# A float residual added by a transposing TensorE pass instead of an identity product

## The chip, the cores and the metric

The kernel runs on one core of a Trainium2 chip. The metric is the device time of one execution in microseconds (us). TensorE (PE, with its weight loads PEld) multiplies, VectorE (DVE) and ScalarE (ACT) work on elements, GpSimd (POOL) too, and SyncE (SP) mostly issues DMA transfers.

## The reference

Four layers follow each other on x of shape (4, 128, 128, 128), all in float32. Each is x = x + layer(groupnorm(x)).

```python
x = x + _L0_conv_ref(_gn(x), ...)   # deformable 3x3 convolution, ReLU
x = x + _L1_conv_ref(_gn(x), W)     # scan over rows: new = row + relu(conv1d(carry, W))
x = x + _L2_conv_ref(_gn(x), ...)   # three products: itself, sum over width, sum over height
x = x + _L3_conv_ref(_gn(x), ...)   # triangle product, below
```

The last layer is the one that matters here:

```python
xn = layer_norm(x, norm_g, norm_b)
left = (xn @ left_w + left_b) * sigmoid(xn @ lgate_w + lgate_b)
right = (xn @ right_w + right_b) * sigmoid(xn @ rgate_w + rgate_b)
out_gate = sigmoid(xn @ ogate_w + ogate_b)
out = einsum('bkjd,bkid->bijd', left, right)
out = layer_norm(out, onorm_g, onorm_b) * out_gate
return out @ to_out_w + to_out_b
```

## The kernel before, in words

The deformable layer runs to about 3050 us of the span, the scan over rows from there to 3931 us, and `message_and_triangle`, which holds layers 2 and 3, from there to the end. Only the last is touched.

In it one image is worked on after the other, in three parts.

- `taken_in(b)`, a generator, reads layer 1's output in strips of eight rows (`x2c`), forms layer 2 into `X` (L1276, L1282, L1285), writes `X` to memory as `x3T` in the layout [channel, row, column], and then normalises it in place: product with a centring matrix (L1316), squares, means (L1331), a round trip through memory for the row factors (`stdT`, `rstd`, `rwide`), and a multiplication on DVE (L1354).
- `multiplied(b)` makes left and right with their gates (L1369, L1374, L1375), the output gate, which goes to memory as `gateT` (L1382 to L1389), and the triangle product into `T` (L1393, L1397).
- `given_out(b, T)`, a generator, yields the output in 32 groups of four rows. DVE takes the statistics of `T` (L1409 to L1423); ACT and POOL normalise to `u` (L1438, L1434). Then, per group: a gate is loaded into `gate` (L1446) and a part of `x3T` into `x3` (L1448); TensorE transposes `u` (L1451); ACT scales it to `y` (L1453); POOL multiplies by the gate (L1454). The sum `po` is then made in PSUM, for each of four columns j: the residual `x3[:, j]` (L1457) opens the sum, the product of `y[:, j]` and `outw` (L1460) closes it. ACT copies `po` into the same `gate` buffer (L1461), and SP writes it out (L1462).

`x3` comes with channels on the partitions, and the output has rows there; so the residual has to be turned on its way into the sum. The kernel before does this with a plain product: `x3[:, j]` as stationary operand and the identity as moving one.

`gate`, `x3`, `y` and `u` have two buffers each; `po` and the transposes share four PSUM banks (`one_ps`); `T` and `X` have one buffer each.

The loop at the end of `message_and_triangle` takes in image 0, and then for each image calls `multiplied(b)` and steps through `given_out(b)` with two steps of `taken_in(b + 1)` after each group. The last image's output thus has nothing beside it. On each engine the instructions are laid in an order that a planner works out from the program; in the trace, the first L1457 of a group stands before the transposes (L1451) of the following one. SP issues the DMAs of all three parts in one queue, in order.

Of the kernel before, what the change touches and what calls it, by code (L numbers as in the profile page):

```python
# [1154 lines left out]
def message_and_triangle(tc, c, x2T, counted, w2, w3, out, x3T, gateT, stdT):  # L1155
# [10 lines left out]
    with ExitStack() as ctx:  # L1166
# [76 lines left out]
        def single(shape=(P, 512)):  # L1243
            return ps_s.tile(list(shape), F32, name="one_ps", tag="one_ps")
# [155 lines left out]
        def given_out(b, T):  # L1400

            prod = T[:, 0:NQ].rearrange("p q d j -> p (q d) j")
            JS = 2 * JB

            def factors(j0):

                st = two.tile([P, JS, 6], F32, name="st")
                for j in range(JS):
                    nc.vector.bn_stats(st[:, j, :], prod[:, :, j0 + j])  # L1409

                both = two.tile([P, JS, 2], F32, name="both")
                nc.vector.tensor_tensor(both, st[:, :, 1:3], st[:, :, 4:6], ALU.add)
                apart = two.tile([P, JS], F32, name="apart")
                nc.vector.tensor_tensor(apart, st[:, :, 1], st[:, :, 4], ALU.subtract)
                nc.vector.tensor_tensor(apart, apart, apart, ALU.mult)
                rs = two.tile([P, JS], F32, name="rs")
                nc.vector.scalar_tensor_tensor(
                    rs, apart, P / 4.0, both[:, :, 1], ALU.mult, ALU.add
                )
                nc.scalar.activation(rs, rs, AF.Sqrt, bias=c.eps, scale=1.0 / P)  # L1420
                nc.vector.reciprocal(rs, rs)
                nm = two.tile([P, JS], F32, name="nm")
                nc.vector.scalar_tensor_tensor(nm, both[:, :, 0], -0.5, rs, ALU.mult, ALU.mult)  # L1423
                return rs, nm

            ready = factors(0)
            for j0 in range(0, S, JB):
                if j0 % JS == 0:
                    rs, nm = ready
                u = two.tile([P, JB, P], F32, name="u")  # L1430
                for j in range(JB):
                    of, k = prod[:, :, j0 + j], j0 % JS + j
                    if j % 4 == 3:
                        nc.gpsimd.tensor_scalar(  # L1434
                            u[:, j], of, rs[:, k : k + 1], nm[:, k : k + 1], ALU.mult, ALU.add
                        )
                    else:
                        nc.scalar.activation(  # L1438
                            u[:, j], of, AF.Identity, bias=nm[:, k : k + 1], scale=rs[:, k : k + 1]
                        )  # L1440
                if j0 % JS == 0 and j0 + JS < S:
                    ready = factors(j0 + JS)
                for h in range(0, JB, 4):
                    j1 = j0 + h
                    gate = two.tile([P, 4, S], F32, name="gate")
                    nc.sync.dma_start(gate, gateT[b, :, j1 : j1 + 4, :])  # L1446
                    x3 = two.tile([P, 4, S], F32, name="x3")
                    nc.sync.dma_start(x3, x3T[b, :, j1 : j1 + 4, :])  # L1448
                    pt = single((P, 4, P))
                    for j in range(4):  # L1450
                        nc.tensor.transpose(pt[:, j], u[:, h + j], c.ident)  # L1451
                    y = two.tile([P, 4, P], F32, name="y")
                    nc.scalar.activation(y, pt, AF.Identity, bias=obcol, scale=ogcol)  # L1453
                    nc.gpsimd.tensor_tensor(y, y, gate, ALU.mult)  # L1454
                    po = single((P, 4, P))
                    for j in range(4):
                        nc.tensor.matmul(  # L1457
                            po[:, j], lhsT=x3[:, j, :], rhs=c.ident, start=True, stop=False
                        )
                        nc.tensor.matmul(po[:, j], lhsT=y[:, j], rhs=outw, start=False, stop=True)  # L1460
                    nc.scalar.copy(gate, po)  # L1461
                    nc.sync.dma_start(out[b, :, j1 : j1 + 4, :], gate)  # L1462
                    yield
# [3 lines left out]
        for b in range(B):  # L1467
            T = multiplied(b)
            after = taken_in(b + 1) if b + 1 < B else iter(())
            for _ in given_out(b, T):  # L1470
                next(after, None)
                next(after, None)
            for _ in after:
                pass
# [75 lines left out]
```

## Time and profile before

| | |
|---|---|
| median of three runs | 5704.68 us (5692.88 to 5705.37) |
| profiled execution, its own time | 5716.77 us |
| its span, first to last instruction | 5715.0 us |
| mean granted TensorE clock | 0.952 |
| PE, PEld busy | 5055.9 us, 4359.9 us |
| DVE, ACT, POOL busy | 3207.3, 2556.8, 1162.6 us |
| L1457 records, weight loads as well | 1024 each, from 4279 to 5711 us |
| L1451 records | 512, from 4279 to 5700 us |

The layer-3 part by stretches, with TensorE's busy time and the mean granted clock:

| stretch, us | what runs | PE busy, us | clock |
|---|---|---|---|
| 4279 to 4463 | output of image 0, intake of image 1 | 143.6 | 0.93 |
| 4463 to 4530 | last groups of image 0, products of image 1 | 51.8 | 0.87 |
| 4530 to 4695 | products of image 1 | 153.5 | 0.98 |
| 5112 to 5296 | output of image 2, intake of image 3 | 145.0 | 0.92 |
| 5365 to 5517 | products of image 3 | 151.5 | 1.00 |
| 5517 to 5715 | output of image 3 alone | 119.6 | 0.72 |

A row of the groups names the line, engine and operation, the tiles written and read, the shapes and the count; then busy time and mean duration of one; then the engine's idle time ahead of them and what ended it. Records of TensorE overlap: a matmul's duration is longer than the step to the next one. The chain of work that ended last is followed back from the last instruction to what released each step. A row of the timeline has start, length, engine, line, operation, and, in brackets, idle time before it.

### The profile page before, as it was taken

The page shows a single profiled execution, that of the slowest core. Times are in us where ns is not written, and L with a number is a line of the kernel's source. Part 1 is how long each engine was busy: PE and PEld are TensorE (multiplying, and loading weights), DVE is VectorE, ACT ScalarE, POOL GpSimd, SP SyncE. Part 2 cuts the span into 40 slices and gives each one's busy share as a digit, 9 for nine tenths or more (in the row PEclk, how much of TensorE's full clock was granted, in tenths as well). Part 3 has the DMA queues.
Part 4 walks back from the last instruction along what each step waited for, and adds up shares of the span by engine and source line. Part 5 has one row for each costly group of instructions (what it writes and reads, how often), then busy time and mean ns, then how long its engine had stood idle before and what let it go on. Part 6 is the DMA issues. An engine that isn't in the chain of part 4 may idle for free. (4 is left out here: it accounts for less than half of the span.)

```text
span 5715.0 us, 163429 instructions
## 1 busy us (share of the span) xinstructions
PE 5055.9 (88%) x69432; PEld 4359.9 (76%) x69432; DVE 3207.3 (56%) x8190; ACT 2556.8 (45%) x5243; POOL 1162.6 (20%) x1013
## 2 busy tenths in 40 slices
PE   2898999999999999899998999997797887887886
PEld 1787788787887888788997999996474774774775
DVE  4666666666666666655555666666446245345350
ACT  1554454544545445445442333331445445446444
POOL 4222222201212012221000111112104204214112
PEclk9999999999999999999998999999999999999987
DMA  4776566665666756556442222222417317327324
GB/s 150 155 166 148 128 148 133 154 132 114 148 135 144 142 103 146 130 125 130 87 92 79 78 87 77 77 87 75 149 49 238 129 66 235 118 79 230 111 70 134
DMA packets 1273820, 710.73 MB, mean 124 GB/s; under 512 B 845645, under 2 KB 1112174, under 8 KB 1263862
## 3 DMA queue, kind: packets, MB, share of 16 engines
q1 hardware_dynamic: 1243538, 658.56, 46.1%
q10 hardware_dynamic: 29540, 41.60, 2.1%
q8 instruction: 549, 8.99, 0.7%
q14 instruction: 193, 1.58, 0.1%
HBM read 417.28 MB, written 282.55 MB: 122 GB/s over the span
## 5 line engine op out<-in xcount | busy, mean ns | idle before, releaser
L606 PE MATMUL conv_ps<-ring,wdef 128*128 128x192 f32 (+2 forms) x7632 | 1295.4, 319 | 5.8 <-DVE x1c L576 4.8
L514 DVE TENSOR_TENSOR m<-t_ps,tent 128x390 f32<-128x390 f32 x1548 | 806.9, 557 | 785.1 <-ACT tent L512 769.2
L606 PEld LDWEIGHTS conv_ps<-ring,wdef 128*128 128x128 f32 x7632 | 1141.5, 194 | 125.3 <-issue 64.0
L512 ACT COPY tent<-t_ps 128x390 f32<-128x390 f32 x1560 | 691.4, 487 | 652.6 <-PE t_ps L498 642.4
L498 PE MATMUL t_ps<-parts_of,spread 57*64 57x99 bf16 (+1 forms) x12384 | 741.7, 275 | 167.2 <-DVE m L514 145.0
L523 PE MATMUL v_ps<-m,pixels 60*64 60x108 f32 (+1 forms) x22704 | 813.7, 265 | 18.4 <-DVE m L514 8.8
L498 PEld LDWEIGHTS <-spread 57*64 57x64 bf16 x12480 | 577.5, 125 | 311.8 <-issue 264.5
L523 PEld LDWEIGHTS v_ps<-m,pixels 60*64 60x64 f32 x22704 | 674.0, 137 | 68.7 <-DVE m L514 23.1
L549 ACT COPY ring<-v_ps 128x432 f32<-128x432 f32 x1032 | 505.7, 525 | 445.1 <-PE v_ps L523 444.4
L420 POOL TENSOR_TENSOR off<-off,koff 72x512 f32<-72x512 f32 x128 | 162.7, 1271 | 1761.8 <-DVE off L417 1761.8
L1369 PEld LDWEIGHTS pair_ps<-wcat,X 128*128 128x128 f32 x4096 | 474.3, 192 | 52.3 <-POOL X L1356 23.2
L1369 PE MATMUL pair_ps<-wcat,X 128*128 128x128 f32 x4096 | 495.9, 279 | 19.8 <-POOL X L1356 18.2
L1375 DVE TENSOR_TENSOR T<-pair_ps,sig 128x512 f32<-128x512 f32 x256 | 266.8, 1043 | 424.1 <-ACT sig L1374 415.5
L1110 PEld LDWEIGHTS own_ps<-diff,wconv 128*128 128x128 f32 x4064 | 494.4, 191 | 13.2
L1110 PE MATMUL own_ps<-diff,wconv 128*128 128x128 f32 x4064 | 495.2, 273 | 0.0
L506 PE MATMUL t_ps<-parts_of,spread 57*64 57x130 bf16 x9288 | 454.2, 225 | 0.0
L1150 POOL TENSOR_TENSOR sum_h<-sum_h,x2c 128x512 f32<-128x512 f32 x128 | 162.5, 1269 | 1137.9 <-DVE x2c L1136 680.4
L438 DVE SCALAR_TENSOR_TENSOR parts<-off,parts 72x512 bf16<-72x512 f32 x384 | 296.1, 772 | 150.7 <-ACT parts L430 145.0
L1460 PE MATMUL one_ps<-outw,y 128*128 128x128 f32 x1024 | 247.6, 334 | 122.5 <-POOL y L1454 122.4
L1068 ACT ACTIVATE rowT<-x1T_ps,t_x,s_x 128x128 f32<-128x128 f32 x512 | 207.7, 568 | 313.2 <-PE x1T_ps L1064 313.2
L1460 PEld LDWEIGHTS one_ps<-outw,y 128*128 128x128 f32 x1024 | 195.2, 239 | 174.5 <-POOL y L1454 172.7
L506 PEld LDWEIGHTS <-spread 57*64 57x64 bf16 x9312 | 318.8, 108 | 0.1
(183 smaller groups left out, 6930.0 us busy)
## 6 DMA issues: line engine op xcount, KB each, us to landing
pixels<-tab SPq DMA_DIRECT2D x688, 123.8 KB
parts_of<-off SPq DMA_DIRECT2D x1032, 55.7 KB
off<-parts SPq DMA_DIRECT2D x64, 891.0 KB
tab<-rows SPq DMA_DIRECT2D x384, 128.0 KB
xin<-in_x_dram SPq DMA_DIRECT2D x128, 256.0 KB
x<-x1c SPq DMA_DIRECT2D x32, 1024.0 KB
x1rows<-x SPq DMA_DIRECT2D x128, 256.0 KB
x2T<-x2c ACTq DMA_DIRECT2D x128, 256.0 KB
```

The source lines that it names most:

```text
L438: nc.vector.scalar_tensor_tensor(parts[:, NSPLIT + i, h : h + RO, 2 : S + 2], off, 0.0, part, ALU.is_gt, ALU.mult,)
L498: nc.tensor.matmul(tp[h : h + HALF, 0, 0:n].rearrange("p (r c) -> p r c", c=PADW)[:, :, i:PADW:RX], lhsT=spread[0:k, kx // 2, i, h : h + H ...
L506: nc.tensor.matmul(tp[h : h + HALF, 1, i * PADW : (i + 1) * PADW], lhsT=spread[HALF : HALF + k, kx // 2, first + i, h : h + HALF], rhs=src ...
L512: nc.scalar.copy(tent[:, 0:n], tp[:, 0, 0:n])
L514: nc.vector.tensor_tensor(m, *pair, ALU.mult)
L523: nc.tensor.matmul(to[p1 : p1 + HALF], lhsT=pix[p0 : p0 + LANES, xb, :], rhs=m[p0 : p0 + LANES, :, RX * xb : RX * xb + w], start=True, sto ...
L549: nc.scalar.copy(to, bodies[side])
L606: nc.tensor.matmul(pc[:, at : at + rows, x0:x1], lhsT=wdef[:, side, k, :], rhs=v[:, :, k if v.shape[2] == NK else kx, x0 + kx : x1 + kx], ...
L1110: nc.tensor.matmul(own[:, n], lhsT=wt[:, 2 * j + n, :], rhs=diffs[h][:, n, :, j : j + V], start=False, stop=(n == 1 and j == NJ - 1),)
L1369: nc.tensor.matmul(pj[:, j], lhsT=X[:, j0 + j, :], rhs=wcat[:, q * 4 * DQ : (q + 1) * 4 * DQ], start=True, stop=True,)
L1375: nc.vector.tensor_tensor(T[:, q : NQ + 1 : NQ - q, :, j0 : j0 + JB], pj[:, :, 0 : 2 * DQ].rearrange("p j (n d) -> p n d j", n=2), sig.rea ...
L1460: nc.tensor.matmul(po[:, j], lhsT=y[:, j], rhs=outw, start=False, stop=True)
```

## The change

One argument is added to the first of the two matmuls that make `po`. The operands, the order, the buffers and everything else stay.

```diff
                     po = single((P, 4, P))
                     for j in range(4):
                         nc.tensor.matmul(
-                            po[:, j], lhsT=x3[:, j, :], rhs=c.ident, start=True, stop=False
+                            po[:, j], lhsT=x3[:, j, :], rhs=c.ident, start=True, stop=False,
+                            is_transpose=True,
                         )
                         nc.tensor.matmul(po[:, j], lhsT=y[:, j], rhs=outw, start=False, stop=True)
```

With it the pass is a transpose of `x3[:, j]` with the identity as the other operand, the form of L1451, and its result is still what the following product adds to.

## The prediction

> **What bounds the kernel now.** I read the page for the whole, then the groups of instructions by line and shape for the prices, the timeline for the true spacing of TensorE's passes, the chain of work that ended last for what lies on the path, and the waits of SP's queue for what is late next.
>
> ```profile
> span 5715.0 us, 163429 instructions
> ...
> PEclk9999999999999999999998999999999999999987
> ```
>
> Each digit is a fortieth of the span, 143 us. The edited line runs from 4279 us on, so only the last eleven or so slices matter: 1436 us after the scan. In the last one and a half the granted clock falls: the windows query gives 0.72 for 5517 to 5715 us, where it gives 0.92 for the earlier output stages and 0.98 for the products between them. A mean of 0.72 between full and half speed means about 55% of that stretch at half speed.
>
> ```profile
> L1460 PE MATMUL one_ps<-outw,y 128*128 128x128 f32 x1024 | 247.6, 334 | 122.5 <-POOL y L1454 122.4
> L1457 PE MATMUL one_ps<-ident,x 128*128 128x128 f32 x1024 | 238.3, 321 | 53.1 <-DMA x<-x3T 51.5 <-ACT gate L1461 1.4
> ...
> L1451 PE MATMUL one_ps<-ident,u 128*128 128x128 f32 x512 | 89.6, 299 | 41.1 <-ACT u L1438 41.0
> ```
>
> The counts are what to see. The source calls each of the three lines 512 times (4 images, 32 groups, 4 columns). L1451, which already transposes, has 512 records; L1457 and L1460, plain float products of the same size, have 1024: two passes each, with two weight loads. The mean of 321 ns is the latency of one pass; passes overlap, so it is not the price. The price is the step from one weight load to the next:
>
> ```profile
> 4482.27 0.55 PEld L1460 LDWEIGHTS one_ps<-outw,y 128*128 128x128 f32 x2
> ...
> 4482.69 0.87 PEld L1451 LDWEIGHTS one_ps<-ident,u 128*128 128x128 f32 x4
> ...
> 4483.54 0.55 PEld L1457 LDWEIGHTS one_ps<-ident,x 128*128 128x128 f32 x2
> ...
> 4483.97 0.87 PEld L1451 LDWEIGHTS one_ps<-ident,u 128*128 128x128 f32 x4
> ```
> ```profile
> 4430.22 0.30 PEld L1460 LDWEIGHTS one_ps<-outw,y 128*128 128x128 f32 x2
> ...
> 4430.44 0.47 PEld L1451 LDWEIGHTS one_ps<-ident,u 128*128 128x128 f32 x4
> ...
> 4430.88 0.30 PEld L1316 LDWEIGHTS pair_ps<-X,cs 128*128 128x128 f32 x2
> ```
>
> The first block is at half clock: two product passes take 4482.69 - 4482.27 = 0.42 us, four transposes 0.85 us, two identity passes 0.43 us: 0.21 us a pass, whatever its kind. The second is at full clock: 0.22 us for two, 0.44 us for four: 0.11 us a pass. Going from products to transposes and back adds nothing in either block.
>
> ```profile
> by line: issue 11.6%; POOL zc L1276 9.7%; DMA rwide<-stdT 9.4%; DVE X L1285 9.3%; DMA gate<-gateT 8.7%; POOL y L1454 6.4%; PE one_ps L1460 4.6%; DVE st L1409 3.8%; ACT u L1438 3.8%; PE one_ps L1457 3.4%; DMA stdT<-rstd 3.2%; DMA out_dram<-g
> ```
> ```profile
> by line: DMA gate<-gateT 21.3%; PE one_ps L1460 20.3%; PE one_ps L1457 13.1%; POOL y L1454 10.3%; DMA out_dram<-gate 9.0%; issue 8.9%; ACT u L1438 4.3%; ACT gate L1461 4.2%; DVE st L1409 4.2%; SPq L1462 1.0%; POOL u L1434 0.5%; PE one_ps L1
> ```
>
> The first is the chain from 4279 to 4463 us, where the output of image 0 runs beside the intake of image 1; it is spread over POOL, DVE and DMA. The second is the last image alone, 5517 to 5715 us: no engine is full, and the path is a ring. One turn of it:
>
> ```profile
> 5599.57 1.27 POOL y L1454
> 5600.89 0.80 PE one_ps L1460 x2
> 5601.68 0.43 PE one_ps L1457 x2
> 5602.11 0.43 PE one_ps L1460 x2
> ...
> 5604.32 0.59 ACT gate L1461
> 5604.93 2.58 DMA out_dram<-gate
> 5607.53 3.15 DMA gate<-gateT
> 5610.84 1.27 POOL y L1454
> ```
>
> There are two gate buffers. A gate is loaded, multiplied on POOL, gone through on TensorE, evicted into the same buffer, written out, and only then is the next gate loaded. TensorE's passes of a group stand in full on this ring, 11.3 us a turn, at half clock. SP's queue, in the stretch from 5510 us, shows the second tie:
>
> ```profile
> SPq L1448 <- PE one_ps L1457: 92.5, 18, 17.1
> SPq L1446 <- DMA out_dram<-gate: 29.6, 21, 2.4
> ```
>
> SP waits with a load of x3 until the last identity product of an earlier group lets the buffer go; the write of the output and the next gate loads are queued behind it.
>
> **What the Trainium skill says.** "TensorE: Matmul & The Clock Gate", Terms, says that the weight load and matmul have a transpose mode, four times faster for FP32. The trace shows half of that: one pass in place of two, each at the same step. The same page, Part 4, puts a transpose in a kernel at about 275 ns and says that transposes do not count as TensorE activity for the full clock. L1451's median record of 273 ns agrees with the first; no run here shows the second, and I keep it as a risk. Its Part 1 gives some 3.4 us of busy time before the clock rises; at 5600.88 us passes start at 0.21 us and reach 0.11 us at about 5604, which agrees. "PSUM — Partial Sum Buffer" (rule 2 on accumulation) says that a float transpose sets the written bits as a product does, so the product can add onto it; the trace before has no such pair.
>
> **The change part by part.** It removes one pass and one weight load from each of 512 identity products. All L1457 weight loads, by the step to the following load, have medians of 112 ns (663 of them) and 213 ns (306), mean 143 ns: 512 x 0.143 = 73 us less TensorE work. That is the ceiling of the direct gain, not the gain. No DMA, buffer, engine or wait is added or moved in the source.
>
> Unshown: a transpose opening a sum that a product then closes. From below: no extra, as at every change between L1451 and products above; no reason speaks for a gain beyond the removed pass. From above: one lost pass per pair, which eats the saving entirely. I take no extra, and keep the upper end as a rival.
>
> What lies on the path: L1457's share of the chain by stretch, times its length. Last image: 13.1% x 198 = 25.9 us. Output beside intake: 3.4% x 184 = 6.3, 4.0% x 195 = 7.8 and 3.4% x 194 = 6.6 us. The remaining groups beside the next image's products (about 68 us each): 7.5%, 7.1% and 9.0%, so 5.0, 4.9 and 6.2 us. The mixed stretches sum to 36.8 us. Half goes: 13.0 us and 18.4 us.
>
> The last image, checked from the ring: after y is ready a group runs 8 product passes and 6 identity passes (the first identity product went ahead); 3 of 14 go, 0.64 us at 0.213. Turns that go through the second group as well lose 6 passes, 1.28 us at half clock, or 0.64 us where the clock had risen. Sixteen turns of 0.64 to 1.28 us are 10 to 20 us; as both buffers have to come round, I keep 13. What is late next there is the gate load itself (3.15 us) and y on POOL: in this turn the second y ends at 5602.87 us (1.27 us from 5601.60) and TensorE, which came to it at 5603.83, would come 0.64 us earlier, so POOL keeps some 0.3 us of slack; much more would not all count.
>
> In the mixed stretches I take 70% of 18.4, 13 us: POOL's zc, DVE's X and the round trips of the row factors stand there beside the ring, and take over some of what is freed. The 70% is a choice; 0% and 150% (x3 buffers free earlier, so SP's queue moves up) are its ends.
>
> Sum: 26 us. The profiled execution took 5716.8 us (1.8 us around the span), which gives 5690.8. It lies 12 us above the median of the runs shown; taken from that, 5704.7 - 26 = 5679 us.
>
> **Rivals.** (a) Hidden in the mixed stretches: only the last image gains, 6 to 13 us, about 5695. For it: no line holds over 12% of that chain; against it: SP waits for L1457 and L1460 there too. (b) Larger: with the queue of SP moving up, the mixed stretches give back more than the chain shows, 50 us in all, 5655. For it speaks that T can't be overwritten before the last group is out. (c) Slower: the order on TensorE is not that of the source (the first identity product of a group stands ahead of the transposes of the next), so a planner that weighs durations lays it, and shorter passes can make it lay SP's queue differently in the mixed stages. The price of one bad place is on the chain:
>
> ```profile
> 4367.01 11.00 DMA gate<-gateT
> ```
>
> A gate load of 11.0 us where others take about 3.2: 8 us. From four of these more (over 26 / 8 = 3.3) the gain is gone; two per mixed stage, six, give 48 - 26 = 22 us slower, 5727. Against it: no duration elsewhere changes. (d) The transpose opening a sum costs a pass more, or is still run as two: 0, 5705.
>
> A clock that sags because transposes do not count would cost part of the last image's 13 us and leaves the case in (a).
>
> **How the numbers follow.** Forecast (17 to 37 us less) 0.50; (a) 0.24; (b) 0.13; (c) 0.09; (d) 0.04. About 0.3%, 17 us, is what a measurement of this kernel can tell from no change. Faster is the forecast and (b), 0.63; same (a) and (d), 0.28; slower (c), 0.09. The range goes from 5648 (most of b) to 5702 (nearly all of a); outside are (c), (d) and the tail of (b), some 0.17.
>
> **What would show it.** L1457 with 512 records, steps of 0.11 and 0.21 us unchanged; L1460 unchanged. Turns in the last image shorter by 0.6 to 1.0 us, its stretch near 185 us. If L1457 keeps 1024 records, (d). If the clock in the last image is clearly under 0.72, the sag. If the last image gains 13 us and the time between first outputs of successive images (417 us) does not fall, (a); if it rises, (c).

## The result, and the profile after

The changed kernel takes 5670.14 us (median of 5 runs, 5668.54 to 5676.25), the kernel before 5704.68 us (5 runs, 5692.88 to 5707.67). The ratio is 0.9947, 95% interval 0.9932 to 0.9962: 30 us less by the ratio (21 to 39 us), 34.5 us by the medians. The profiled execution took 5676.25 us, with a span of 5674.5 us.

The page of the changed kernel, first its span and its granted clock:

```profile
span 5674.5 us, 162404 instructions
...
PEclk9999999999999999999998999999998998998997
```

There are 1025 instructions less: 512 passes, as many weight loads, and one other on balance. The groups by line and shape (out<-in, shapes, count | busy us, mean ns | idle before). The new argument has a source line of its own, so the closing product, L1460 before, is L1461 here, the eviction L1462 and the write L1463:

```profile
L1461 PE MATMUL one_ps<-outw,y 128*128 128x128 f32 x1024 | 236.3, 337 | 140.1 <-POOL y L1454 140.0
...
L1457 PE MATMUL one_ps<-ident,x 128*128 128x128 f32 x512 | 164.2, 321 | 47.0 <-DMA x<-x3T 38.4 <-ACT gate L1462 5.2 <-ACT y L1453 1.6
L1451 PE MATMUL one_ps<-ident,u 128*128 128x128 f32 x512 | 91.2, 296 | 41.3 <-ACT u L1438 41.2
```

L1457 has 512 records where it had 1024, as L1451 has. Its mean of 321 ns has not moved, which shows again that the mean is a latency and not the price. The price is in the timeline, here at half clock in the last image (start, length, engine, line):

```profile
5613.03 0.23 PEld L1457 LDWEIGHTS one_ps<-ident,x 128*128 128x128 f32 x1
5613.25 0.55 PEld L1461 LDWEIGHTS one_ps<-outw,y 128*128 128x128 f32 x2
5613.67 0.23 PEld L1457 LDWEIGHTS one_ps<-ident,x 128*128 128x128 f32 x1
5613.89 0.55 PEld L1461 LDWEIGHTS one_ps<-outw,y 128*128 128x128 f32 x2
```

One residual pass takes 0.22 us, the two product passes behind it 0.42 us. A column costs 0.64 us where it cost 0.85 us, and the change between the two kinds of pass, now twice in every column, adds nothing. Over the whole kernel the step from an L1457 weight load to the next load has medians of 112 ns at full and 213 ns at half clock, before and after (steps with idle time in them left out).

Where the time went is read by stages, each from the last triangle product of one image to that of the next, and to the end. The windows of the kernel before (stretch, length, busy time of PE, PEld, DVE, ACT, POOL, granted clock, share of DMA, GB/s):

```profile
4268.00:4684.00 416.00, 348.91 (x2195) 269.63 (x2194) 188.87 (x356) 206.67 (x341) 105.77 (x96) 0.94 0.43 142
4684.00:5102.00 418.00, 353.26 (x2196) 273.76 (x2194) 188.25 (x356) 207.13 (x342) 107.25 (x96) 0.93 0.44 142
5102.00:5516.00 414.00, 349.78 (x2188) 270.32 (x2189) 189.42 (x355) 206.15 (x340) 105.75 (x96) 0.94 0.43 140
5516.00:5715.00 199.00, 120.20 (x646) 109.96 (x644) 50.40 (x176) 93.91 (x171) 58.11 (x64) 0.72 0.41 124
```

and of the changed kernel:

```profile
4273.00:4678.00 405.00, 335.20 (x2066) 252.68 (x2066) 195.22 (x356) 208.64 (x343) 103.23 (x96) 0.94 0.44 147
4678.00:5086.00 408.00, 340.53 (x2067) 257.80 (x2066) 193.08 (x356) 209.04 (x343) 102.71 (x96) 0.93 0.44 145
5086.00:5492.00 406.00, 338.10 (x2065) 253.60 (x2064) 191.63 (x355) 205.97 (x340) 104.24 (x96) 0.92 0.43 143
5492.00:5674.00 182.00, 100.39 (x513) 88.41 (x512) 50.09 (x176) 93.44 (x170) 58.16 (x64) 0.72 0.44 135
```

The first three stages, called mixed here since an output runs beside an intake, are 8 to 11 us shorter each. The last is 16 us shorter (198.4 to 182.5 us, unrounded). What lies ahead of these stages is 5 us longer. ACT and POOL are busy for about as long as before, DVE 2 to 6 us longer in each mixed stage. The clock of the last image is 0.72 in both. Single profiles of this kernel scatter: an experiment below has mixed stages with nothing changed in them that sum to 1232 us, where the profile of before has 1248. So the split is settled by timed experiments and not by these two tables.

The chain of the last image, by line, and one turn of it:

```profile
by line: DMA gate<-gateT 23.8%; PE one_ps L1461 17.9%; POOL y L1454 12.8%; DMA out_dram<-gate 12.5%; issue 8.1%; PE one_ps L1457 6.2%; ACT gate L1462 4.9%; DVE st L1409 4.5%; ACT u L1438 3.5%; DMA x<-x3T 1.4%; SPq L1463 0.9%; POOL u L1434 0
```
```profile
5600.58 1.27 POOL y L1454
5601.90 0.79 PE one_ps L1461 x2
5602.69 0.21 PE one_ps L1457
5602.90 0.43 PE one_ps L1461 x2
...
5607.04 0.59 ACT gate L1462
5607.65 0.34 SPq L1463
5608.04 3.14 DMA gate<-gateT
5611.34 1.27 POOL y L1454
...
5614.98 2.63 DMA x<-x3T
...
5619.20 3.07 ACT u L1438 x6
...
5622.42 1.27 POOL y L1454
```

L1457 had 13.1% of 198 us, 25.9 us, and has 6.2% of 182 us, 11.3 us. The turn from 5600.58 to 5611.34 takes 10.8 us, the next 11.1 us; in the kernel before, the turns from y at 5599.57 and at 5610.84 us took 11.3 and 12.3 us. New in the second turn are the load of x3 and, behind it, the normalisation of the next u on ACT: the gate no longer ends last there. This is so in one turn only, the load of x3 has 1.4% of the chain. In the first turn the gate load leaves right behind SP's issue of the other group's write (`SPq L1463`), and not behind the landing of a write: SP's order is a part of the ring, too.

SP's queue in the last image:

```profile
SPq L1448 <- PE one_ps L1457: 82.8, 18, 16.4
SPq L1446 <- DMA out_dram<-gate: 29.0, 24, 2.4
```

SP's longest wait is still the one for the residual passes: 82.8 us in 182 where it was 92.5 in 205. It has about the same share of the stretch as before.

### The profile page after: what moved, and what is told of

It is laid out like the page before. It is cut to its first block, busy times and chain, and to the rows that moved or that the text cites. A ratio compares the mean times of both kernels' runs of the same rounds, so it can differ in the third digit from the quotient of the medians.

```text
span 5674.5 us, 162404 instructions
## 1 busy us (share of the span) xinstructions
PE 5005.7 (88%) x68920; PEld 4294.2 (76%) x68920; DVE 3220.7 (57%) x8190; ACT 2558.2 (45%) x5247; POOL 1153.9 (20%) x1013
## 5 line engine op out<-in xcount | busy, mean ns | idle before, releaser
L1461 PE MATMUL one_ps<-outw,y 128*128 128x128 f32 x1024 | 236.3, 337 | 140.1 <-POOL y L1454 140.0
L1461 PEld LDWEIGHTS one_ps<-outw,y 128*128 128x128 f32 x1024 | 197.2, 241 | 185.1 <-POOL y L1454 182.0
```

## The experiments

Theory P: the gain comes from the number of TensorE passes on the path alone, in the last image by the ring of the gate buffers, in the mixed stages by the part that lies on the chain. Rival O: the planner laid a new order (it did: from the first mixed stage on, engines have other orders than before), and part of the gain is the order's. Rival K: it is the kind of pass, or the clock's answer to it, and not the number. Each ratio below is of timed runs against the kernel before on the same chip, with its 95% interval; the microseconds are the ratio less one, times the median of before there (5710 to 5716 us). Three chips were used, so two of these runs are compared through their ratios.

**Order and passes apart.** Whether a matmul is a transpose can be set after the planner has laid the order. Before's order with the new passes, and the new order with before's passes, are then two clean halves: in the traces DVE, ACT, POOL and SP run in the order of the kernel before in the first, and in that of the changed kernel in the second. The last two arguments are the flag and the number of residual passes, counted from the last, that it is given to. A residual pass is found as a product that opens a sum and has the identity as an operand; there are 512. The code is cut at the dots:

```diff
+def turned_after_planning(nc, flag, count):
...
+    for block in nc.main_func.blocks:
+        for k, ins in enumerate(block.instructions):
...
+            if ins.start_tensor_calc and not ins.stop_tensor_calc and "in=[dt.float32@ident" in str(ins):
+                found.append((block, k))
...
+    for block, k in found[-count:]:
+        block.instructions[k] = block.instructions[k].__replace__(is_transpose=flag)
...
     with _tile.TileContext(nc) as tc:
         tile_preact_convs(tc, *args)
+    turned_after_planning(nc, True, 512)
```

Old order, transposes:

> The order of every engine is that of the kernel before; the residual passes are turned into transposes only after the planner has laid it. Theory P (the shorter passes alone do it, on the ring and on SP's queue): 28 to 36 us less than before, as the whole change. Theory O (the planner's new order brings the surplus of the mixed stretches over half of the chain's share): 15 to 22 us less, of which 13 to 16 in the last image. If the order were the whole of it: only the last image's 13 to 16 us.

Measured: 0.9939 (0.9919 to 0.9959), 35 us less. Its last image:

```profile
5504.00:5689.00 185.00, 104.12 (x516) 91.65 (x514) 50.08 (x176) 93.69 (x171) 58.20 (x64) 0.70 0.44 133
```

The passes alone, under an order that was laid for the dearer ones, give the whole effect of the change (0.9947). The interval, 23 to 46 us, leaves out the 15 to 22 us of theory O.

New order, products (the changed kernel with the flag taken back in all 512):

> The opposite part: the order of the changed kernel, with the residual passes turned back into plain products after planning. Theory P: within 5 us of before. Theory O: 10 to 18 us less than before, all in the mixed stretches; the last image as before, near 198 us.

Measured: 0.9984 (0.9974 to 0.9994), 9 us less (3 to 15). The last image:

```profile
5513.00:5713.00 200.00, 119.97 (x648) 109.81 (x647) 50.03 (x176) 94.17 (x171) 58.17 (x64) 0.73 0.41 124
```

So the new order is worth a little by itself with the old passes, between what the two theories said, and nothing in the last image. It does not visibly add to the passes: the old order with the new passes is no slower than the changed kernel. Under the new order the passes are worth some 21 us by these ratios (30 less 9), under the old one 35, and the intervals don't tell these apart. That the order alone makes the gain is excluded; that it has a few us of it is not.

**Where the passes pay.** The old order, with the flag for the 128 residual passes of the last image only:

```diff
+    turned_after_planning(nc, True, 128)
```

> Order of before, transposes only in the 128 residual passes of the last image. Both theories: 13 to 16 us less than before, all of it after the last triangle product (stretch of 198 us to about 183 us), since the ring of the gate buffers carries it. If the last image gained because the earlier images left things in another state: under 5 us.

Measured: 0.9965 (0.9953 to 0.9977), 20 us less (13 to 27).

```profile
5509.00:5694.00 185.00, 103.91 (x520) 91.54 (x518) 50.25 (x176) 94.16 (x171) 57.98 (x64) 0.70 0.44 134
```

The last image takes 185 us where it took 199, 14 us less. Nothing is changed in the mixed stages, and two of them came out at 409 us in this profile against 418 and 414 in the one of before: that is the scatter.

The old order, with the flag for the first 384 passes (`found[:-128]`), the three mixed stages:

> Order of before, transposes in the 384 residual passes of the first three images and plain products in the last. If the mixed stretches gain by the shorter passes alone: what the run with all 512 under the old order had (about 35 us less) minus what the last image alone had (14 to 20), so 13 to 21 us less, the last image at 198 to 200 us as before. If their gain were noise of single profiles: under 6 us.

Measured: 0.9977 (0.9966 to 0.9987), 13 us less (7 to 19).

```profile
5500.00:5698.00 198.00, 118.17 (x642) 107.61 (x640) 51.85 (x176) 93.59 (x170) 58.00 (x64) 0.75 0.41 124
```

The last image is at its old length. 20 and 13 us make 33, beside 35 for both together: within their intervals the parts add, as they should if each stage gains by its own passes. The chain agrees: summed over the three mixed stages the residual passes have 36.7 us of it in the profile of before, 15 us here, and 19 us in the changed kernel.

**Number or kind.** The changed kernel with every residual transposed twice into the same place, the first of the two serving nothing, so that two passes stand where two product passes stood:

```diff
                     for j in range(4):
+                        nc.tensor.transpose(po[:, j], x3[:, j, :], c.ident)
                         nc.tensor.matmul(
```

> The changed kernel with each residual transposed twice into the same place (the second opens the sum), so two passes stand again where before had two. Theory that only the number of passes counts: the whole gain goes, within 8 us of before, the last image at 196 to 201 us and its share of half clock as before (about 0.55). Rival, that transposing passes do not count as activity for the clock: the share of half clock in the last image rises to 0.65 or more and the time is 5 to 15 us above before. Rival, that it is the kind of pass and not their number: still 20 us or more less than before.

Measured: 1.0025 (1.0016 to 1.0034), 14 us slower than before (9 to 19).

```profile
5525.00:5725.00 200.00, 118.22 (x655) 107.55 (x653) 48.61 (x176) 94.42 (x172) 58.19 (x64) 0.73 0.41 124
```

The whole gain is gone, and the last image is where it was, at the same clock: 0.73 beside 0.72, which is about 54% of the stage at half clock beside 56%. K falls for the last image, for the kind of pass and for the clock. The time itself met neither expectation cleanly: 14 us are more than the 8 us that theory P allowed, and the 5 to 15 us that K named came without its sign in the clock. Where these 14 us lie isn't shown. The mixed stages of this profile sum to 1251 us beside 1248, within the scatter; the kernel has a new order and 512 more instructions to lay, and which of these costs the time was not separated.

**Is it the ring?** Two kernels take something else off the ring. First, the changed kernel with the finished sum evicted into `y`, whose reading is over by then, and written from there. A gate load then waits only for POOL and no longer for a write:

```diff
-                    nc.scalar.copy(gate, po)
-                    nc.sync.dma_start(out[b, :, j1 : j1 + 4, :], gate)
+                    nc.scalar.copy(y, po)
+                    nc.sync.dma_start(out[b, :, j1 : j1 + 4, :], y)
```

> The changed kernel, but the finished sum is evicted into the y buffer and written out from there, so a gate load no longer waits for the write of the group two before it. Theory that the ring gate load - y - TensorE - eviction - write bounds the last image: a turn loses the load of about 3.2 us in 10.8, the last image falls from 183 to 140 to 155 us and the whole by 25 to 60 us. Rival (TensorE at half clock, ACT and POOL in series bound it, or SP's queue): under 10 us less.

Measured: 0.9860 (0.9833 to 0.9888), 80 us less than before, so some 50 us less than the changed kernel, with nothing added.

```profile
5480.00:5643.00 163.00, 91.93 (x517) 80.03 (x515) 44.82 (x176) 94.05 (x171) 58.36 (x64) 0.76 0.49 151
```
```profile
by line: PE one_ps L1461 22.3%; POOL y L1454 11.7%; DMA x<-x3T 11.5%; issue 10.5%; DMA out_dram<-y 10.4%; PE one_ps L1457 10.2%; DVE st L1409 5.1%; POOL u L1434 4.1%; PE one_ps L1451 4.0%; ACT y L1453 2.3%; ACT u L1438 2.0%; ACT y L1462 1.8
```

The first line is the last image's window, the second its chain. The gate load, 23.8% of the chain in the changed kernel, is no longer on it. The 50 us are in the expected range, but the last image is only 20 us shorter, where at least 28 were expected: the load of x3 takes the place of the gate, with 11.5%. So the ring of the gate buffers was the bound of the last image, and another ring stood close behind. The other 30 us, by the ratio, are not in the last image. The mixed stages of this profile sum to 1205 us beside 1219 in the changed kernel, no more than their scatter, so where they lie is not shown, nor how much is due to the new order that the planner lays for this edit.

The same with plain products:

> The kernel before (plain products) with the finished sum written out from the y buffer. Against the same with transposes (1.4% less than before, 80 us): theory that TensorE's passes stay on the new path (x3 load - TensorE - y - TensorE): still 25 to 35 us slower than that one, so 45 to 55 us less than before. Rival, that with the gate load gone from the ring TensorE's passes are hidden behind transfers: within 10 us of it.

Measured: 0.9888 (0.9867 to 0.9908), 64 us less than before, the last image at 170 us.

```profile
5481.00:5651.00 170.00, 109.33 (x646) 97.31 (x645) 43.77 (x176) 95.01 (x171) 58.18 (x64) 0.82 0.47 145
```

Beside the 80 us of the run with transposes the passes are worth some 16 us here, half of what they are worth with the gate ring; the intervals of the two overlap, and the planner's orders differ too, so the 16 is rough, and neither the 25 to 35 us of the one theory nor the "hidden" of the other came out clearly. In the last image the passes are worth 7 us (170 to 163) where they were worth 14 to 16. The granted clock there is higher in the dearer kernel, 0.82 with products and 0.76 with transposes; these are single profiles.

Second, the changed kernel with all four residual passes of a group ahead of its four products, so that none stands between y and the eviction. Only the first pass has `start=True`; the other three write into other columns of the same bank without it:

```diff
                     for j in range(4):
                         nc.tensor.matmul(
-                            po[:, j], lhsT=x3[:, j, :], rhs=c.ident, start=True, stop=False,
-                            is_transpose=True,
+                            po[:, j], lhsT=x3[:, j, :], rhs=c.ident, start=j == 0,
+                            is_transpose=True, stop=False, skip_group_check=True,
                         )
-                        nc.tensor.matmul(po[:, j], lhsT=y[:, j], rhs=outw, start=False, stop=True)
+                    for j in range(4):
+                        nc.tensor.matmul(
+                            po[:, j], lhsT=y[:, j], rhs=outw, start=False, stop=True, skip_group_check=True,
+                        )
```

> The changed kernel with all four transposes of a group ahead of its four products, so that none of them stands between y and the eviction. Theory ring: the three passes still on the ring in the last image go, 0.64 us a turn at half clock, 16 turns: about 10 us there; x3's buffer also comes free before y is ready, which takes SP's wait for it away, so 10 to 30 us less than the changed kernel in all. Rival (the wait only moves to the next load): under 5 us less.

Measured: 0.9953 (0.9937 to 0.9969), no better than the change itself (0.9947). The expectation of theory ring failed and the rival's number came. The window and the chain of the last image say where, and so do the waits of SP's queue, first two of this kernel and then one of the changed kernel:

```profile
5493.00:5692.00 199.00, 111.17 (x518) 97.56 (x517) 45.62 (x176) 93.58 (x171) 58.48 (x64) 0.65 0.39 124
```
```profile
by line: DMA gate<-gateT 25.7%; PE one_ps L1462 19.9%; issue 12.1%; POOL y L1454 9.9%; ACT gate L1465 8.0%; PE one_ps L1451 6.1%; ACT u L1438 5.1%; DVE st L1409 4.1%; SPq L1466 2.6%; PE one_ps L1457 2.1%; POOL u L1434 0.5%; SPq L1448 0.5%; 
```
```profile
SPq L1466 <- ACT gate L1465: 98.6, 24, 5.6
SPq L1448 <- PE one_ps L1457: 29.8, 16, 4.4
```
```profile
SPq L1463 <- ACT gate L1462: 27.1, 32, 6.0
```

The residual passes are off the path, 2.1% of it, as intended. SP waits less for them, 29.8 us in place of 82.8. But the stage is 199 us long, and three things came with the edit. SP now waits with the write at the head of its queue until ACT has evicted the sum, 98.6 us in place of 27.1, and the next gate loads stand behind that write: no landing of a write is on this chain any more, the gate loads follow on SP's issue. The planner lays the transposes of the next groups (L1451, 6.1% of the chain) between the products of two groups, so that the second group's products wait for them. And the granted clock is 0.65. How much each of the three costs was not separated.

With both edits together:

> Both: transposes ahead of the products, and the output from the y buffer. If the load of x3, which waits for the last transpose of the group two before, is what bounds the last image with the output from y: the last image falls from 163 to 130 to 150 us, the whole by 20 to 50 us against that run. Rival (ACT's u and POOL's y in series): under 10 us.

Measured: 0.9893 (0.9871 to 0.9914), 61 us less than before, behind the 80 us of the output from y alone (the intervals, 49 to 74 and 64 to 95 us, overlap); the last image at 160 us beside 163. The load of x3 is off the chain of the last image, where it had 11.5%, and little came of it: the products have 27.5% of the chain there where they had 22.3%, y on POOL 17.7% where it had 11.7%, and the clock is 0.69 where it was 0.76. So either the rival held, with the work in series behind the load, or the clock and the order took the gain back.

At last the output from y, issued by ACT:

```diff
-                    nc.sync.dma_start(out[b, :, j1 : j1 + 4, :], y)
+                    nc.scalar.dma_start(out[b, :, j1 : j1 + 4, :], y)
```

> The output written from the y buffer as in the run that had 1.4% less than before, and issued by ACT right behind its eviction, so that SP's queue holds loads only. If SP's waits for the eviction (26 us in the last image) hold loads back: 10 to 30 us less than that run, 1.6 to 1.9% less than before. If the loads wait for their buffers anyway: within 6 us of it.

Measured: 0.9918 (0.9902 to 0.9933), 47 us less than before, 33 us behind the same with SP's queue. Neither expectation came.

```profile
by line: DMA out_dram<-y 24.2%; PE one_ps L1461 23.8%; DMA x<-x3T 10.6%; PE one_ps L1457 9.2%; POOL y L1454 8.9%; DVE st L1409 4.8%; issue 4.1%; PE one_ps L1451 2.7%; ACT u L1438 2.3%; ACT y L1462 2.3%; ACT y L1453 2.2%; PE one_ps L1393 1.2
```

The write has 24.2% of the last image's chain where it had 10.4%: y waits for it. One reading is that SP's queue, freed of the eviction, sends its loads ahead and they crowd the write on which the next y waits; no run settles it. It also covers the smaller part: in the profiles the last image is 6 us longer than with SP's queue, so most of the 33 us must lie in the mixed stages (1221 us together beside 1205), and what costs them is open.

## Why the prediction was right

Its forecast was 26 us less; the ratio gives 30 (21 to 39). The steps, one by one:

- *One pass in place of two, at an unchanged step.* Right: 512 records, 112 and 213 ns. The unshown pair, a transpose that opens a sum, costs nothing extra; the upper bound of a lost pass did not come.
- *13 us in the last image from half of L1457's share of its chain.* Right, somewhat low: 16 us between the two profiles, 14 us in the stage of the kernel with only these passes changed, 20 us (13 to 27) by its ratio. What the ring gave, 0.64 to 1.28 us in a turn, is seen as 0.5 and 1.2 us. The passes' time on this chain fell from 25.9 to 11.3 us, by a little more than half.
- *13 us in the mixed stages, 70% of half of the chain's share.* The number came; the 70% is not shown. The 18.4 us that it is taken of fit the two profiles: the passes' time on the chain of these stages fell by 17.5, from 36.7 to 19.2 us. With those 384 passes alone the kernel gained 13 us, but the interval, 7 to 19, reaches from 40% to all of 18.4. The prediction called the 70% a choice, and that it met the middle is luck as far as these runs can tell. The two profiles show 29 us there (415.9, 417.5 and 414.7 to 405.0, 407.8 and 405.9 us), and would have spoken for the rival of the larger gain. But the run with only the last image changed shows 16 of these 29 us with nothing changed in its mixed stages.
- *What is late next.* Named were the gate load and y on POOL. POOL's slack was there (the second y ends at 5603.54 us, and TensorE comes to it about 0.6 us later). The x3 load, which the prediction saw in SP's queue but not as the next on the ring, came up in one turn of the changed kernel, and with 11.5% of the chain once the gate ring was cut. The prediction also let every gate load wait for the landing of a write; in some turns, before the change too, it waits for SP to issue the other group's write.
- *Rival (c), a new order of the planner that costs more than it saves.* The order did change; with the old passes it saved 9 us. The twice transposed kernel and the one with residuals first have other orders too, and lose 14 us to before, or the gain they were built for; an order that costs would fit both, but it was not shown in either.
- *The sag of the clock* because transposes do not count (the Trainium skill, "TensorE: Matmul & The Clock Gate", Part 4): not seen in the last image. The clock is 0.72 before and after. With every residual transposed twice it is 0.73, although that stage has half the product passes of before in the same time. The 3.4 us after which the prediction saw the clock rise are those of one turn: the passes that start at 5612.15 us in the kernel before are still at 0.21 us a pass 5 us later.

## What to carry to other kernels

An element-wise residual that has to be turned on its way into PSUM costs one float pass as a transpose and two as a product with the identity, and the sum that follows adds onto it without extra cost; so it was here, at 128 x 128 in float32. What that is worth is not the 73 us of engine time but the share of it on the chain, stage by stage. Half the chain's share was a good estimate where a ring of buffers carried the stage; where POOL, DVE and DMA ran beside it, the gain lay somewhere between 40% and all of that. Before shortening what stands on a ring, ask whether the ring can be cut: evicting into a buffer whose reading was already over gave 64 us on the kernel before, twice what the transposes gave, and was found by reading which load waited for which write.

## What the runs showed of the hardware

A float product of 128 x 128 by 128 columns is two passes of 0.11 us at full clock and 0.21 us at half clock, a float transpose one of the same length. The Trainium skill, "TensorE: Matmul & The Clock Gate", Terms, gives the transpose mode a factor of four for FP32; here it is two.

The granted clock of the last image did not follow the number of TensorE passes alone. With the gate ring it was 0.72, 0.73 and 0.75 in three profiles with plain residual passes and 0.70, 0.70 and 0.72 in three with transposes; with the output from y it was 0.82 and 0.76. With the residuals ahead of the products it was 0.65 with the gate ring and 0.69 with the output from y, at as many passes as in the runs with 0.72 and 0.76. What sets it isn't shown here.
